# Attention over 4 images of 4096 positions: v's forms by halves of the channels, two products of the next step ahead of the second pair of banks, the projection one step behind

## The chip, the core and the metric

The kernel runs on one core of one Trainium2 chip. Its engines work side by side and wait for each other through semaphores: TensorE (PE) multiplies matrices, VectorE (DVE) and ScalarE (ACT) work on elements, GpSimd (POOL) and SyncE (SP) here mostly issue DMAs. TensorE writes its sums into eight PSUM banks; the other data lies in SBUF or, between stages, in DRAM. The metric is the device time of one execution in microseconds (us); three runs of the kernel before gave 2387.89, 2389.86 and 2392.86 us, median 2389.86.

## The reference

x is (4, 64, 64, 256), float32. Three projections give q and k with 128 channels and v with 256. Note that the results are only reshaped, not transposed, ahead of the attention, so a "channel" of the attention is a stretch of the flattened image.

```python
N = W * H                                   # 4096
q = jnp.einsum('bwhc,cd->bwhd', x, Wq) + bq # 128 channels
k = jnp.einsum('bwhc,cd->bwhd', x, Wk) + bk # 128 channels
v = jnp.einsum('bwhc,cd->bwhd', x, Wv) + bv # 256 channels
pq, pk, pv = (t.reshape(B, -1, N) for t in (q, k, v))
energy = jnp.einsum('bcn,bcm->bnm', pq, pk)
attention = jax.nn.softmax(energy, axis=-1)
out = jnp.einsum('bcm,bnm->bcn', pv, attention).reshape(B, W, H, C)
return gamma * out + x
```

## The kernel before

**Numbers in three forms.** Float32 data goes through TensorE as float32r. Each matrix is split into three forms, h (upper part), l (rest) and d (h scaled up a little, less the matrix). A product needs the d form's product, scaled by ScalarE, and on top the h and l forms' products. `split` (L153), `x_forms` (L212), `qk_forms` (L301) and `halves` (L389) make forms: ScalarE makes h, then VectorE d and l.

**Steps.** The attention of an image is cut into 8 groups (`NG`) of 512 columns n, and each group into 16 steps (`NU`) of two blocks of 128 rows m: 128 steps (`STEPS`) an image, 512 in all. The loop from L695 runs over these steps; n is the step, t its place in its group, b the image, and `late` says that the last image is reached (n >= 384). All instructions are put down by hand (the pools are under a manual schedule); each engine runs its own in that order. One iteration n issues, in this order:

- `cross(n + 2)` (L356): one matmul of the d forms for each of the two blocks (L362), scaled in its bank by ScalarE (L363). Two banks, tag "e", serve all steps.
- at t = 0, `upper(n + 1)`, ScalarE's h of the next step (L386), which the last step of a group leaves out; at t = 15, `sum_forms` (L455): ScalarE writes the h form zf of the group's sum (L460), VectorE its l form later (L462).
- ScalarE's part of a projection piece, `step(p, "act")`.
- `attend(n, 0)` (L422): six matmuls (L434). It multiplies v by the step's exps. j = 0 and 1 are the halves of the result's rows; each has a pair of PSUM banks, a (h and l forms) and b (d form), in which it adds up over the 16 steps of a group. So the first step of a group must find its four banks emptied.
- `energy(n + 2)` (L365): the h and l products on top of cross, four matmuls (L377), then ScalarE's exps (L380).
- `load_k(n + 5)` on POOL's queue and `store()` on SP's, which issues what is in the list `stores`.
- at t = 0 of images 0 to 2, `emptied(n - 1, 1)`: ScalarE copies the second pair of banks of the old group to SBUF (L448); at t = 15 `emptied(n, 0)` for the first pair. Otherwise `upper(n + 2)`.
- TensorE's part of the projection piece; at t = 0 `sums` of the old group (L472, two matmuls, and a copy by ScalarE, L473), and the generator `finish` (L475) is started, which each iteration takes one piece further: the sum to DRAM and back (SP, L480 and L482), its reciprocal at t = 3, back through DRAM, two operations of VectorE, at t = 8 a DMA on POOL's queue that adds x (L498), at t = 11 the store of the output on SP's queue (L502).
- `halves(n + 1)` on VectorE: the running sum (L397), l (L411) and d (L413); then VectorE's part of the projection piece.
- `attend(n, 1)`, six matmuls.
- at t = 6 a load of q, and at n = 115 to 130 of each image but the last a load of v of the next image into vall, which holds v for all 16 steps (`load_v`, L336), both on POOL's queue.

**Projection of the next image.** While an image is attended, the next one is projected in pieces (`step`, L563). 16 pieces r = 0 to 15 (`R`) serve one pair of blocks, 8 pairs an image; p counts the pieces, and r is p mod 16. r = 0: transposes; 1 to 4: forms of x; 5 and 6: products for q and k; 7 to 10: their forms; 9 to 12: products for v, first one half of its channels (eh = 0), then the other; 11 to 14: v's forms; 12 also loads the next x (SP). Each form is stored in DRAM by SP in the iteration after it is done: qk's after r = 8 and r = 10 (four DMAs of 192 KB each time), v's after r = 12 and r = 14 (two of 384 KB each time). At L714 p is n - 3 for n < 17, then two pieces an iteration for n = 17 to 23, then n + 4, so r = t + 4.

**Buffers that matter here.** The tag "pf" of the pool `work` has two buffers in turn: for the two forms of q and k, the two of v, and zf, five in each group. Whoever writes into such a buffer waits until the DMAs that store its old content are through. "o", the group's result before its store, has one buffer; "ld" (l and d) has two.

Of the kernel before, what the change touches and what calls it, by code (L numbers as in the profile page):

```python
# [9 lines left out]
F32 = mybir.dt.float32  # L10
F32R = mybir.dt.float32r
# [9 lines left out]
def kernel(  # L21
# [37 lines left out]
    B, W, H, C = x.shape  # L59
    P = 128  # L60
# [24 lines left out]
    NU = NM // 2  # L85
    STEPS = NG * NU
# [14 lines left out]
    with ExitStack() as fast:  # L101
# [4 lines left out]
        qkv = pool("qkv", 1)  # L106
        ppool = pool("ppool", 2)
        work = pool("work", 2)
        kpool = pool("kpool", 3)
        dram = pool("dram", 2, space=DRAM)  # L110
# [2 lines left out]
        ps_o = pool("ps_o", 1, space=PSUM)  # L113


        vall = qkv.tile([P, NU, 3, 2, C], F32R, tag="v", name="v")
        wf = qkv.tile([P, 2, 3, KC, C], F32R, tag="wf", name="wf")
        zd, rd = (dram.tile([B * NG, NB], F32, tag=n, name=n, bufs=1) for n in ("zd", "rd"))
        xs4 = work.tile([P, 4, 2, XB], F32, tag="o", name="xs", bufs=1)
# [25 lines left out]
        qd, kf, vf, units, loads, now = {}, {}, {}, {}, {}, {}  # L145
        active, stores = [], []
# [6 lines left out]
        def split(h, l, d, y):  # L153

            nc.scalar.activation(h, y, AF.Identity, scale=UPPER * E)  # L155
            yield
            for t, f in ((d, 1.0 / E + 1.0), (l, 1.0 / E)):
                nc.vector.scalar_tensor_tensor(t, h.bitcast(F32), -f, y, ALU.mult, ALU.add)  # L158
                yield
# [12 lines left out]
        def image(b):  # L172
            for g in range(NG):
                qd[b, g] = dram.tile([P, NJ, 3, P], F32, tag=f"qd{g}", name=f"qd_{b}_{g}")
            for t in range(NU):
                kf[b, t] = dram.tile([P, 2, 3, P], F32, tag=f"kf{t}", name=f"kf_{b}_{t}")
                vf[b, t] = dram.tile([P, 3, 2, C], F32, tag=f"vf{t}", name=f"vf_{b}_{t}")

        def bank(name, shape, b, ring):
            if b:  # L180
# [10 lines left out]
        def load_x(b, i):  # L191
            if b == B or i >= NI:
                return
            if b == 0:
                t = xs4[:, i % 4]
                if i:
                    nc.sync.dma_start(t, xv[b, i])
                loads["x", b, i] = t
                return
            pair = work.tile([P, 2, 2, XB], F32, tag="xd", name=f"x_{b}_{i}", bufs=1)  # L200
            for u in range(2):
                nc.sync.dma_start(pair[:, u], xv[b, i + u])
                loads["x", b, i + u] = pair[:, u]
# [115 lines left out]
        def v_forms(i):  # L319
            y = units.pop((1, 0, i))  # L320
            units.pop(("xf", 0, i))
            yield from split(vall[:, i, 0], vall[:, i, 1], vall[:, i, 2], y)

        def v_pair_forms(b, i, eh):
            y = units.pop(("v", b, i, eh))
            f = work.tile([P, 3, 2, C], F32R, tag="pf", name=f"vf{eh}_{b}_{i}")
            yield from split(f[:, 0], f[:, 1], f[:, 2], y)
            for u in range(2):
                stores.append((vf[b, i + u][:, :, eh, :], f[:, :, u, :]))

        def store():
            for to, f in stores:
# [3 lines left out]
        def load_v(b, t):  # L336
            nc.gpsimd.dma_start(vall[:, t], vf[b, t])
# [18 lines left out]
        def cross(n):  # L356

            if n >= B * STEPS:
                return
            for i in range(2):  # L360
                e = units["e", n, i] = ps_e.tile([P, NB], F32, tag="e", name=f"e_{n}_{i}")
                nc.tensor.matmul(e, *forms(n, i, 2), start=True, stop=False, skip_group_check=True)  # L362
                nc.scalar.mul(e, e, -REST)  # L363

        def energy(n):  # L365

            if n >= B * STEPS:
                return
            if n % NU:
                x = ppool.tile([P, 2, NB], F32, tag="x", name=f"x_{n}")  # L370
            else:
                x = ppool.tile([P, 2, NB], F32, tag="s", name=f"s_{n // NU}")
            units[n] = x
            for i in range(2):
                e = units.pop(("e", n, i))
                for f in range(2):
                    nc.tensor.matmul(  # L377
                        e, *forms(n, i, f), start=False, stop=(f == 1), skip_group_check=True
                    )
                nc.scalar.activation(x[:, i, :], e, AF.Exp, scale=(1.0 + E) ** 3 / E)  # L380

        def upper(n):
            if n >= B * STEPS:
                return
            h = ppool.tile([P, 2, NB], F32R, tag="h", name=f"h_{n}", bufs=3)
            nc.scalar.activation(h, units[n], AF.Identity, scale=UPPER)  # L386
            units[n] = units[n], h
# [34 lines left out]
        def attend(n, j, order=(0, 1, 2)):  # L422

            t = n % NU
            if t == 0:
                for i, c in enumerate("ab"):
                    pool, tag = ps_o, f"{c}{j}"
                    if j and n >= (B - 1) * STEPS and n // NU % 2 == 0:
                        pool, tag = now["banks"][i]
                    now[c, j] = pool.tile([P, NB], F32, tag=tag, name=f"{c}{j}_{n // NU}")  # L430
            for f in order:
                to = now["ab"[f == 2], j]
                for i in range(2):
                    nc.tensor.matmul(  # L434
                        to,
                        vall[:, t, f, i, j * P : (j + 1) * P],
                        units[n][f][:, i, :],
                        start=(t == 0 and i == 0 and f != 1),
                        stop=(t == NU - 1 and i == 1 and f != 0),
                        skip_group_check=True,  # L440
                    )
# [13 lines left out]
        def sum_forms(n):  # L455

            s = now["total"] = now["sum"]
            f = work.tile([P, 2, NB], F32R, tag="pf", name=f"zf_{n // NU}")
            h, l = now["z"] = f[:, 0, :], f[:, 1, :]
            nc.scalar.activation(h, s[:, 0, :], AF.Identity, scale=UPPER)  # L460
            yield
            nc.vector.tensor_tensor(l, s[:, 0, :], h.bitcast(F32), ALU.subtract)  # L462
            yield
# [231 lines left out]
        for n in range(B * STEPS):  # L695
            b, u = divmod(n, STEPS)
            g, t = divmod(u, NU)
            final = n == B * STEPS - 1
            if n == 0:
                image(1)  # L700
                load_x(1, 0)
            if u == STEPS - 5 and b + 2 < B:
                image(b + 2)
            if n == B * STEPS - 6:
                xr = ppool.tile([P, 2, NB], F32, tag="s", name="xr")
                nc.sync.dma_start(xr, xg[b, g])
            cross(n + LOOK)
            turn = t == NU - 1 and not final
            if t == 0 and n:
                upper(n + LOOK - 1)  # L710
            if turn:
                zf = sum_forms(n)
                next(zf)
            p = n - 3 if n < 17 else 2 * n - 20 if n < 24 else n + 4  # L714
            step(p, "act")
            if not final:
                attend(n, 0)
            energy(n + LOOK)
            load_k(n + LOOK + 3)
            store()  # L720
            late = n >= (B - 1) * STEPS
            if t == 0 and n:
                done = full
            if t == late and n > 1:
                emptied(n - 1 - late, 1, done)
            if turn:
                emptied(n, 0)
            else:
                upper(n + LOOK)
            step(p, "pe")  # L730
            if t == 2 * late and n > 2:
                sums(n - 1 - 2 * late)
                active.append(finish(n // NU - 1, now["o"], now["total"]))
            halves(n + 1)
            if turn:
                next(zf)
            step(p, "dve")
            if final:
                finish_last(n, xr)
                break  # L740
            attend(n, 1)
            full = now["a", 1], now["b", 1]
            if 17 <= n < 24:
                for engine in ("act", "pe", "dve"):
                    step(p + 1, engine)
            if t == 6 and n + NU < B * STEPS:
                load_q(*divmod(n // NU + 1, NG))
            if n >= STEPS - NU + 3 and (n - 3) // NU % NG == NG - 1 and (n - 3) // STEPS + 1 < B:
                load_v((n - 3) // STEPS + 1, (n - 3) % NU)
            proceed()  # L750
# [5 lines left out]
    with tc.If(nc.values_load(again[0:1, 0:1]) > 0), ExitStack() as general:  # L756
# [3 lines left out]
        xpool, xtpool, qkv = pool("gx", 2), pool("gxt", 2), pool("gqkv", 1)  # L760
        ppool, work = pool("gp", NP + 2), pool("gw", 1)
# [86 lines left out]
        for b in range(B):  # L848
# [16 lines left out]
            for g in range(NG):  # L865
                ps = []
                mx = work.tile([P, 2, NB], F32, tag="mx", name=f"gmx_{b}_{g}")
                for t in range(NP):
# [9 lines left out]
                    p = ppool.tile([P, 2, NB], F32, tag="p", name=f"gp_{b}_{g}_{t}")  # L878
# [54 lines left out]
                for s in range(2):  # L933
                    y = work.tile([P, NB], F32, tag="y", name=f"gy_{b}_{g}_{s}")
# [33 lines left out]
```

## Time and profile before

| | |
|---|---|
| median of 3 runs | 2389.86 us |
| the profiled execution's own time | 2388.01 us |
| its span | 2385.8 us |
| mean granted clock of TensorE | 0.997 |
| DVE busy | 2128.5 us (89%) |
| ACT busy | 1861.9 us (78%) |
| DMA queue q0 (POOL's issues) | 280.67 MB, 44.1% of the 16 engines' span |
| DMA queue q1 (SP's issues) | 130.77 MB, 16.1% |

How to read the profile's lines: a group of instructions is given by its line in the kernel, engine, operation and "output<-input", then shapes and count, busy us, mean ns of one, and the idle time of its engine just ahead of it with what ended it. In the rows in order of time the first two numbers are the start and the duration in us, and the bracket is idle time ahead. A row of the view by stretches has the stretch and its length, then the busy us of PE, PE's weight loads, DVE, ACT and POOL (with counts), TensorE's granted clock, the DMA engines' busy share and GB/s. A row of the chain of waits has start, duration and what the time went to. A matmul of 512 columns is listed with some 390 ns, but the next one starts 227 ns later, since they overlap.

### The profile page before, as it was taken

What the parts mean: (1) busy time and instruction counts of PE and PEld (TensorE: products, weight loads), DVE (VectorE), ACT (ScalarE), POOL (GpSimd) and SP (SyncE); (2) the same over time, 40 slices, a digit from 0 to 9 for tenths busy, and PEclk for the clock granted to TensorE, in tenths of its full rate; (3) what the DMA queues carried; (4) which work ended last, traced back from release to release, by engine and by line L of the source; (5) the groups of instructions that cost most, each with busy time, mean ns of one, the idle gap of its engine ahead of it and who ended that gap; (6) DMA issues with size and microseconds to landing.
All of it is one profiled execution on the core that took longest, in us unless ns stands there. A gap on an engine that the chain in (4) does not pass through costs nothing.

```text
span 2385.8 us, 31624 instructions
## 1 busy us (share of the span) xinstructions
PE 2341.1 (98%) x10844; PEld 1944.8 (82%) x10844; DVE 2128.5 (89%) x2114; ACT 1861.9 (78%) x3042; POOL 355.7 (15%) x642
## 2 busy tenths in 40 slices
PE   9999999999999999999999999999999999999998
PEld 9877888888878888888887888888888888888887
DVE  8988999889888899988988889999899888888888
ACT  7777878778777787877877778777787788887885
POOL 1101111111211111111121111111112111111110
PEclk9999999999999999999999999999999999999999
DMA  8456665556875666555688456665569644444453
GB/s 277 152 146 178 184 183 146 138 163 190 285 234 144 171 184 183 152 137 160 188 296 250 135 158 185 183 168 146 144 179 331 189 126 120 128 130 112 132 135 95
DMA packets 210382, 413.81 MB, mean 173 GB/s; under 512 B 26851, under 2 KB 114151, under 8 KB 210214
## 3 DMA queue, kind: packets, MB, share of 16 engines
q0 software_dynamic: 94272, 280.67, 44.1%
q1 hardware_dynamic: 115390, 130.77, 16.1%
q8 instruction: 89, 1.46, 0.3%
q14 instruction: 79, 0.65, 0.1%
q10 hardware_dynamic: 552, 0.26, 0.0%
HBM read 306.64 MB, written 104.98 MB: 173 GB/s over the span
## 4 chain that ended last, share of the span: by engine, by line
PE 86%; ACT 7%; DMA 4%; DVE 2%; issue 1%; SPq 0%; POOL 0%; ACTq 0%; DVEq 0%; POOLq 0%
PE a L434 35%; PE b L434 17%; PE e L377 17%; PE e L362 9%; PE qv L247 4%; PE v L264 2%; ACT x L380 2%; ACT o L448 2%; DMA out_dram<-o 2%; ACT e L363 1%; ACT h L386 1%; PE xt L210 1%; DMA qd<-f 1%; DMA o<-in_x_dram 0%; DVE ld L413 0%
## 5 line engine op out<-in xcount | busy, mean ns | idle before, releaser
L380 ACT ACTIVATE x<-e 128x512 f32<-128x512 f32 x960 | 522.2, 596 | 315.2 <-PE e L377 315.2
L411 DVE TENSOR_TENSOR ld<-x,h 128x1024 fp32r<-128x1024 f32 x480 | 585.4, 1220 | 109.8 <-ACT h L386 57.5
L397 DVE TENSOR_TENSOR s<-s,x 128x1024 f32<-128x1024 f32 x480 | 586.1, 1221 | 96.9 <-ACT x L380 93.9
L434 PE MATMUL a<-h,v 128*128 128x512 f32 x2048 | 637.1, 392 | 27.4 <-ACT o L448 27.4
L363 ACT ACTIVATE e<-e 128x512 f32<-128x512 f32 x1024 | 547.2, 573 | 132.5 <-PE e L362 132.1
L434 PE MATMUL b<-ld,v 128*128 128x512 f32 x2048 | 631.6, 390 | 0.2
L434 PE MATMUL a<-ld,v 128*128 128x512 f32 x2048 | 631.7, 390 | 0.0
L413 DVE SCALAR_TENSOR_TENSOR ld<-h,x 128x1024 fp32r<-128x1024 f32 x480 | 584.4, 1217 | 0.0
L349 POOL DMA_DIRECT2D k<-kf x512 | 272.6, 532 | 1969.0 <-PE e L377 1804.9
L377 PE MATMUL e<-q,k 128*128 128x512 f32 x2048 | 550.0, 390 | 2.4 <-ACT e L363 1.2
L386 ACT ACTIVATE h<-x 128x1024 fp32r<-128x1024 f32 x480 | 510.9, 1064 | 13.3
L434 PEld LDWEIGHTS a<-h,v 128*128 128x128 f32 x2048 | 377.9, 188 | 110.7 <-ACT o L448 38.2
L377 PEld LDWEIGHTS e<-q,k 128*128 128x128 f32 x2048 | 383.2, 188 | 86.6 <-ACT e L363 7.8
L434 PEld LDWEIGHTS b<-ld,v 128*128 128x128 f32 x2048 | 384.4, 188 | 82.2 <-DVE ld L413 1.1
L434 PEld LDWEIGHTS a<-ld,v 128*128 128x128 f32 x2048 | 384.7, 188 | 81.0
L362 PE MATMUL e<-q,k 128*128 128x512 f32 x1024 | 316.4, 390 | 0.9 <-ACT x L380 0.8
L362 PEld LDWEIGHTS e<-q,k 128*128 128x128 f32 x1024 | 191.9, 188 | 42.5 <-ACT x L380 2.3
L311 DVE SCALAR_TENSOR_TENSOR f<-f,qv 128x512 fp32r<-128x512 f32 x128 | 85.5, 678 | 1.2 <-ACT f L308 0.7
L247 PE MATMUL qv<-wf,xf 128*128 128x256 f32 x576 | 80.1, 287 | 2.5 <-DVE xf L229 2.3
L247 PEld LDWEIGHTS qv<-wf,xf 128*128 128x128 f32 x576 | 75.3, 193 | 5.8 <-DVE xf L229 2.5
L158 DVE SCALAR_TENSOR_TENSOR vf<-vf,v 128x512 fp32r<-128x512 f32 x96 | 65.2, 680 | 7.7 <-ACT vf L155 7.7
L411 DVE TENSOR_TENSOR ld<-s,h 128x1024 fp32r<-128x1024 f32 x32 | 39.2, 1226 | 20.1 <-ACT h L386 19.1
(91 smaller groups left out, 1125.2 us busy)
## 6 DMA issues: line engine op xcount, KB each, us to landing
k<-kf POOLq DMA_DIRECT2D x512, 384.0 KB, 3.5
vf<-vf SPq DMA_DIRECT2D x96, 384.0 KB
v<-vf POOLq DMA_DIRECT2D x48, 768.0 KB, 8.3
kf<-f SPq DMA_DIRECT2D x128, 192.0 KB
qd<-f SPq DMA_DIRECT2D x128, 192.0 KB
q<-qd POOLq DMA_DIRECT2D x31, 768.0 KB, 6.6
o<-in_x_dram POOLq DMA_DIRECT2D x31, 512.0 KB, 8.2
out_dram<-o SPq DMA_DIRECT2D x31, 512.0 KB
```

The costliest lines, as they stand in the source:

```text
L247: nc.tensor.matmul(to[:, s, :], left, right.rearrange("p s a -> p (s a)") if w else right, start=(f == 2 and s == k == 0), stop=(f == 1 an ...
L311: nc.vector.scalar_tensor_tensor(f[:, :, :, j, :], h.bitcast(F32), s, y, ALU.mult, op)
L349: nc.gpsimd.dma_start(t, kf[b, u % NU])
L362: nc.tensor.matmul(e, *forms(n, i, 2), start=True, stop=False, skip_group_check=True)
L363: nc.scalar.mul(e, e, -REST)
L377: nc.tensor.matmul(e, *forms(n, i, f), start=False, stop=(f == 1), skip_group_check=True)
L380: nc.scalar.activation(x[:, i, :], e, AF.Exp, scale=(1.0 + E) ** 3 / E)
L386: nc.scalar.activation(h, units[n], AF.Identity, scale=UPPER)
L397: nc.vector.tensor_tensor(s, s, x, ALU.add)
L411: nc.vector.tensor_tensor(l, x, h.bitcast(F32), ALU.subtract)
L413: nc.vector.scalar_tensor_tensor(d, h.bitcast(F32), 1.0 + E, x, ALU.mult, ALU.subtract)
L434: nc.tensor.matmul(to, vall[:, t, f, i, j * P : (j + 1) * P], units[n][f][:, i, :], start=(t == 0 and i == 0 and f != 1), stop=(t == NU - ...
```

## The change

It has three parts. First, v and its forms are laid out with the half of the channels ahead of the form, in vall, in the buffer in which the forms are made and in DRAM. Second, in the first step of a group (t = 0, images 0 to 2, not n = 0) the four matmuls of the h and l forms of step n + 1 into the first pair of banks are issued ahead of attend(n, 1); step n + 1 then issues only its d products there. Third, the piece p of the projection is n - 3 for n < 7, n - 2 for n = 7 to 17 and n - 1 from n = 18 on; only n = 6 and n = 17 run two pieces. From n = 18 on, r is t - 1 (15 at t = 0). Up to L715 the lines keep their numbers, so all that the profile names inside the helpers stay as they are.

```diff
-        vall = qkv.tile([P, NU, 3, 2, C], F32R, tag="v", name="v")
+        vall = qkv.tile([P, NU, 2, 3, C], F32R, tag="v", name="v")
...
-                vf[b, t] = dram.tile([P, 3, 2, C], F32, tag=f"vf{t}", name=f"vf_{b}_{t}")
+                vf[b, t] = dram.tile([P, 2, 3, C], F32, tag=f"vf{t}", name=f"vf_{b}_{t}")
...
         def v_forms(i):
             y = units.pop((1, 0, i))
             units.pop(("xf", 0, i))
-            yield from split(vall[:, i, 0], vall[:, i, 1], vall[:, i, 2], y)
+            yield from split(*(vall[:, i, :, f] for f in range(3)), y)

         def v_pair_forms(b, i, eh):
             y = units.pop(("v", b, i, eh))
-            f = work.tile([P, 3, 2, C], F32R, tag="pf", name=f"vf{eh}_{b}_{i}")
-            yield from split(f[:, 0], f[:, 1], f[:, 2], y)
+            f = work.tile([P, 2, 3, C], F32R, tag="pf", name=f"vf{eh}_{b}_{i}")
+            yield from split(*(f[:, :, j] for j in range(3)), y)
             for u in range(2):
-                stores.append((vf[b, i + u][:, :, eh, :], f[:, :, u, :]))
+                stores.append((vf[b, i + u][:, eh], f[:, u]))
...
                     nc.tensor.matmul(
                         to,
-                        vall[:, t, f, i, j * P : (j + 1) * P],
+                        vall[:, t, i, f, j * P : (j + 1) * P],
                         units[n][f][:, i, :],
...
-            p = n - 3 if n < 17 else 2 * n - 20 if n < 24 else n + 4
+            p = n - 3 + (n > 6) + (n > 17)
             step(p, "act")
-            if not final:
+            late = n >= (B - 1) * STEPS
+            if t == 1 and n > 1 and not late:
+                attend(n, 0, (2,))
+            elif not final:
                 attend(n, 0)
             energy(n + LOOK)
             load_k(n + LOOK + 3)
             store()
-            late = n >= (B - 1) * STEPS
...
+            if t == 0 and n and not late:
+                attend(n + 1, 0, (0, 1))
             attend(n, 1)
             full = now["a", 1], now["b", 1]
-            if 17 <= n < 24:
+            if n in (6, 17):
                 for engine in ("act", "pe", "dve"):
                     step(p + 1, engine)
```

## The prediction

> **What bounds the kernel now.** I read the page first, then the list of waits, then the rows in order of time around one start of a group, then the stretches that differ from it.
>
> ```profile
> PE 2341.1 (98%) x10844; PEld 1944.8 (82%) x10844; DVE 2128.5 (89%) x2114; ACT 1861.9 (78%) x3042; POOL 355.7 (15%) x642
> ...
> PE 86%; ACT 7%; DMA 4%; DVE 2%; issue 1%; SPq 0%; POOL 0%; ACTq 0%; DVEq 0%; POOLq 0%
> ...
> L434 PE MATMUL a<-h,v 128*128 128x512 f32 x2048 | 637.1, 392 | 27.4 <-ACT o L448 27.4
> ```
>
> TensorE is the bound: it is idle for 2385.8 − 2341.1 = 44.7 us. Of these 27.4 us stand ahead of one group, the h products of attend, and ScalarE's emptying of the banks (L448) ends them. No matmul is added or taken away, so only idle time and a lowered clock can be won.
>
> ```profile
> PE a L434 <- ACT o L448: 27.4, 25, 4.7
> ...
> ACT vf L155 <- DMA qd<-f: 7.8, 4, 2.8
> ...
> ACT o L448 <- DMA out_dram<-o: 7.1, 2, 5.1
> ```
>
> The columns are total, times and longest: 25 waits, one of 4.7 us. ScalarE itself waits twice for the store of the output (7.1 us). An ordinary start of a group, n = 176, in order of time:
>
> ```profile
> 886.96 0.62 PE L362 MATMUL e<-q,k 128*128 128x512 f32 x2
> ...
> 888.42 0.62 ACT L460 ACTIVATE zf<-s 128x512 fp32r<-128x512 f32 x1
> ...
> 889.43 1.09 ACT L380 ACTIVATE x<-e 128x512 f32<-128x512 f32 x2 [0.39 <-PE e L377]
> ...
> 891.04 0.62 PE L362 MATMUL e<-q,k 128*128 128x512 f32 x2
> ...
> 892.53 1.08 ACT L386 ACTIVATE h<-x 128x1024 fp32r<-128x1024 f32 x1
> ...
> 893.65 1.23 DVE L411 TENSOR_TENSOR ld<-x,h 128x1024 fp32r<-128x1024 f32 x1 [1.39 <-ACT h L386]
> 893.77 0.63 PE L472 MATMUL z<-zf,ones 128*128 128x512 f32 x2
> ...
> 894.48 0.69 ACT L448 ACTIVATE o<-a,gam 128x512 f32<-128x512 f32 x1
> ...
> 895.05 0.70 ACT L448 ACTIVATE o<-b,gam 128x512 f32<-128x512 f32 x1
> 895.23 0.73 PE L434 MATMUL a<-h,v 128*128 128x512 f32 x2 [0.82 <-ACT o L448]
> ...
> 896.57 0.56 ACT L473 COPY s<-z 1x512 f32<-1x512 f32 x1
> 896.72 0.61 PE L362 MATMUL e<-q,k 128*128 128x512 f32 x2
> 897.14 1.07 ACT L363 ACTIVATE e<-e 128x512 f32<-128x512 f32 x2
> ...
> 898.53 1.07 PE L377 MATMUL e<-q,k 128*128 128x512 f32 x4
> ```
>
> Each step begins with the two matmuls of L362. The last step of the old group lasts 891.04 − 886.96 = 4.08 us for 18 matmuls, 0.227 each. The first step of the new one lasts 896.72 − 891.04 = 5.68 us; it has two more matmuls (sums, L472), so 4.53 us of work and **1.15 us lost**. From 889.43 to 897.14 ScalarE has no idle time of its own: exps, two emptyings, two of L363, h, two exps, two emptyings. The second pair of banks is its last item.
>
> **The early product order.** attend(n+1, 0, (0,1)) puts four matmuls, 0.91 us, between the sums and attend(n, 1); step t = 1 then issues only the d pair there. It needs two things. h of n+1 ends at 892.53 + 1.08 = 893.6, in time. l of n+1 is the VectorE row at 893.65, which had waited 1.39 us for that h; it ends at 894.88. The sums end at 894.23 (893.77 plus two matmuls), the h pair at 894.68, so the l pair waits until about 894.93: 0.25 us. attend(n, 1) then begins at 895.38, after the a bank is free (895.17, and the row at 895.23 was its release) and its b matmuls come well after 895.75. So the old wait ends before it is reached. What is late next: cross(n+3) falls at 895.38 + 1.36 = 896.74, as before, but only the d pair (0.45 us) now stands between it and energy(n+3), where six matmuls stood. The first product ends 0.39 later plus hand-over, ScalarE is free at 897.14, its rescaling of the first bank takes half of 1.07 and ends at 897.75 to 897.8. energy could go at 896.74 + 0.45 + 0.45 = 897.65 and waits to about 897.8, with 0.05 more for the second bank. Lost after the change: 0.25 + 0.2 = 0.45 us; gained 1.15 − 0.45 = 0.70 per start. Bounds: 0 lost (all 1.15 won), or 0.85 lost if every hand-over on the way h, l, PE and PE, ScalarE, PE takes 0.1 more (0.3 won). I take 0.70, since each end is a row's end. The branch runs at n = 16 to 368, 23 starts; without n = 16, 128 and 256, which have troubles of their own, 20 × 0.70 = **14.0 us** (6 to 23).
>
> **The projection's new place, early steps.**
>
> ```profile
> 142.32 4.33 DMA vf<-vf
> ...
> 146.76 0.60 ACT vf L155
> ...
> 148.96 1.19 PE a L434 x4
> ...
> 181.22 6.63 DMA qd<-f
> ...
> 189.10 1.21 PE e L377 x4
> ```
>
> ```profile
> 120.00:180.00 60.00, 56.35 (x263) 46.43 (x261) 51.65 (x55) 45.62 (x76) 6.85 (x13) 1.00 0.50 145
> 180.00:240.00 60.00, 57.96 (x268) 47.43 (x268) 51.54 (x52) 45.23 (x75) 7.58 (x14) 1.00 0.62 178
> 780.00:840.00 60.00, 59.18 (x276) 49.22 (x275) 53.12 (x54) 47.40 (x79) 8.01 (x14) 1.00 0.56 157
> 660.00:720.00 60.00, 54.51 (x242) 44.75 (x241) 48.30 (x49) 42.36 (x70) 9.61 (x17) 0.94 0.75 224
> 1260.00:1320.00 60.00, 57.58 (x264) 47.81 (x265) 52.86 (x53) 45.92 (x75) 9.62 (x17) 1.00 0.80 236
> 1800.00:1860.00 60.00, 59.86 (x264) 49.12 (x263) 54.43 (x52) 48.48 (x80) 16.25 (x31) 1.00 1.07 370
> ```
>
> The chain shows that at 142 and 181 ScalarE's L155 waits for stores to leave the ring of two "pf" buffers. The second wait comes from the doubled steps 17 to 23, in which a buffer is asked for one step after its store. The new rule doubles only n = 6 (DVE pieces) and n = 17 (an empty piece and transposes), so that wait goes. The first stays: zf of n = 15 is still put in between the first two v forms, whose second is asked for at n = 15 instead of 16, and waits for a store of 4.33 us. Idle in the two stretches is 3.65 + 2.04 = 5.69 us (the second column is PE busy); 0.82 of it is the start at n = 32, counted above, and I leave 2 us for the first wait. **2.9 us** won (0 to 4.5).
>
> **The projection's new place, every group.** Piece r falls on t = r + 1 instead of r − 4, with all its DMAs. zf, which ScalarE writes at t = 15, now takes the buffer of the first v form, whose two stores SP issues after VectorE's piece at t = 13; before it had eight steps. That is the added wait, and ScalarE's exps, emptyings and the next rescalings are queued behind it.
>
> ```profile
> 881.35 0.68 DVE L229 SCALAR_TENSOR_TENSOR xd<-xf,xt 128x512 fp32r<-128x512 f32 x1
> ```
>
> This piece at t = 13 stands where the new one will; it ends at 882.0, two issues follow within 0.65 us, and zf goes at 888.42, with 0.39 us of idle behind it. The store has 888.8 − 882.65 = 6.2 us. The rows above give 4.33 us for such a store and 6.63 for one in a fuller queue. I take no wait; bounds 0 and 0.4 us × 23 = 9 us lost.
>
> **The layout.** vall and the forms exchange two axes: the store of a form's half has 128 runs of 3 KB, not 384 of 1 KB. The forms are written in two runs of 256 columns. L311 already writes in runs of 128:
>
> ```profile
> L311 DVE SCALAR_TENSOR_TENSOR f<-f,qv 128x512 fp32r<-128x512 f32 x128 | 85.5, 678 | 1.2 <-ACT f L308 0.7
> ...
> L158 DVE SCALAR_TENSOR_TENSOR vf<-vf,v 128x512 fp32r<-128x512 f32 x96 | 65.2, 680 | 7.7 <-ACT vf L155 7.7
> ```
>
> 678 against 680 ns: nothing. attend reads the same 128 columns.
>
> **The turns of image, n = 128, 256, 384.** Here 16 loads of v share the DMA engines with the stores.
>
> ```profile
> 643.93 24.08 DMA out_dram<-o
> ...
> 668.37 0.70 ACT o L448
> ```
>
> ```profile
> q0 software_dynamic: 1130, 4.64, 75.9%
> q1 hardware_dynamic: 1486, 1.63, 33.7%
> ```
>
> The second view is the queues' packets, MB and share from 644 to 660 us. Before, the output's store stood behind both v forms (1536 runs of 1 KB) on SP, took 24.08 us and stopped ScalarE until 668.37. The stretch from 660 lost 5.49 us idle and had the clock at 0.94, 0.06 × 60 = 3.6 us more: 9.1. The second turn lost 2.42, the third 0.14. After the change the output's store stands behind one q/k form (512 runs) and should be in time; but then the second q/k form, x and both v forms follow, and zf at n = 127 wants the first v form away within some 6 us. In q1's share, 1486 runs in 16 us or 93 a microsecond, the q/k form (512), x (512) and v form (256) are 1280 runs or 13.8 us from about 646, so 660 at best, 665 if larger runs take longer, against zf at 661. I put 5 us on the first turn, 4 on the second, and 1 on the third, which loads no x: 9.1 + 2.4 + 0.1 − 10 = **1.6 us** won (−14 to +10: all three as bad as the first was, or all as good as an ordinary start).
>
> The Trainium skill (DMA: Bandwidth & Descriptors, section Queues, rings and completion order) says that a DMA engine goes round its queues packet by packet, a packet being several descriptors. The near-equal counts of q0 and q1 agree; by it runs three times as long would carry three times the bytes a turn, which is rival B below.
>
> A stall here has a second price: the 0.94 above. The Trainium skill (TensorE: Matmul & The Clock Gate, section What's actually happening) says that about 3.4 us idle halves TensorE's clock; this trace's 4.7 us wait with its clock of 0.94 agrees, and by it a turn that still stalls that long keeps its 3.6 us.
>
> **Sum.** 14.0 + 2.9 + 1.6 = 18.5 us from the profiled execution's 2388.0 (span 2385.8): 2369.5. The median of the runs is 1.9 above that execution, so **2371 us**.
>
> **Rivals.**
> A, the sum above: 2371, alone 2361 to 2382. Chance 0.60.
> B, the turns clear as well, because the 3 KB stores leave in a third of the turns: 10 instead of 1.6, so 2363. For it: the packet counts. Against it: the DMA engines are already full there (75.9 + 33.7%), and the moved stores meet the end of the v loads. Chance 0.17.
> C, the change doesn't take the stall away: ScalarE's run from 889.43 to 897.14 remains, and the wait only moves to l and to energy. With 0.85 to 1.15 lost the starts give 0 to 6 us: 2379 to 2385. Chance 0.12.
> D, slower: zf waits at t = 15 of every group for the first v form's store. Each microsecond past the 6.2 above costs 23 us, and it decides from 18.5 / 23 = 0.8 us, a store of 7.0 us. At 8.2 us the time is 2371 + 46 = 2417. For it: 6.63 us in the early row; against it: the middle of a group has the DMA only half busy (0.56 in the row from 780). Chance 0.08. The other 0.03 is spread.
>
> This kernel's measurement can tell 0.2%, 4.8 us, from no change. A, B and half of C are faster: 0.83. The other half of C is the same, with a little of A and D: 0.09. D and the rest slower: 0.08. The range takes B in and the worse end of C: 2357 to 2386.
>
> **What would show it.** Right: the wait of L434 for L448 falls from 27.4 us to under 3; in its place small waits of L434 for L411 or L413 and of L377 for L363, 0.2 us each at 20 places; the busy PE in ordinary stretches rises from 59.18 to about 59.6; nothing at 181. Wrong: zf (L460) with idle time ended by the store of vf; a wait of L448 that stays; a lower clock in other stretches than now; stalls of k's loads behind the last loads of v.

## The result and the profile after

| | before | after |
|---|---|---|
| median of the runs | 2390.31 us (6 runs, 2387.76 to 2392.86) | 2381.43 us (6 runs, 2379.29 to 2382.37) |
| the profiled execution, its span | 2388.01, 2385.8 us | 2379.29, 2377.4 us |
| mean granted clock of TensorE | 0.997 | 0.996 |

The ratio is 0.9962, interval [0.9949, 0.9975]: 8.9 us faster, where some 19 us were forecast. The time lies inside the stated range of 2357 to 2386.

The page of the kernel after, busy time, the chain's shares, the queue of SP and the two groups of L434 on bank a:

```profile
PE 2353.2 (99%) x10844; PEld 1942.8 (82%) x10844; DVE 2134.5 (90%) x2114; ACT 1861.4 (78%) x3042; POOL 355.2 (15%) x642
...
q1 hardware_dynamic: 90814, 130.77, 15.7%
...
PE 88%; ACT 5%; DMA 3%; DVE 3%; issue 1%; SPq 0%; ACTq 0%; DVEq 0%
...
L434 PE MATMUL a<-ld,v 128*128 128x512 f32 x2048 | 634.7, 391 | 1.2 <-DVE ld L411 0.3
L434 PE MATMUL a<-h,v 128*128 128x512 f32 x2048 | 635.7, 392 | 0.1
```

The 27.4 us ahead of the h products are 0.1. TensorE is idle for 2377.4 − 2353.2 = 24.2 us, 20.5 less than before, yet the span is only 8.4 us shorter. The same 10844 matmuls are listed as 12.1 us busier. A matmul is listed with 390 ns though the next one can start after 227, so a wait of up to some 0.16 us between two of them shows no idle time at all, a longer one shows only its rest, and a lowered clock counts as busy too. Idle time alone does not tell the gain. The bytes of q1 are the same 130.77 MB. The list of waits of after (total, times, longest):

```profile
PEld e L377 <- ACT e L363: 19.9, 62, 0.6
...
ACT vf L155 <- DMA qd<-f: 12.4, 6, 3.3
...
PEld a L434 <- DVE ld L411: 10.5, 21, 0.7
ACT zf L460 <- DMA vf<-vf: 8.0, 3, 3.8
PE e L362 <- ACT x L380: 6.8, 4, 2.8
...
PEld a L434 <- ACT o L448: 1.8, 5, 0.4
```

The store of the output no longer stops ScalarE (it was 7.1 us), and the wait for L448 is nearly gone. New are the 21 waits for l, about one a start, the 62 for L363 (18 with 7.8 us before, so about two more a start), and three of zf for the store of a v form. A weight load's wait partly overlaps the matmul ahead, so these totals are not lost time.

An ordinary start, n = 176, after, in order of time:

```profile
880.21 0.62 PE L362 MATMUL e<-q,k 128*128 128x512 f32 x2
...
882.82 1.23 DVE L411 TENSOR_TENSOR ld<-x,h 128x1024 fp32r<-128x1024 f32 x1 [1.39 <-ACT h L386]
...
883.42 0.63 PE L434 MATMUL a<-h,v 128*128 128x512 f32 x2
...
884.10 0.73 PE L434 MATMUL a<-ld,v 128*128 128x512 f32 x2
...
884.67 0.63 PE L434 MATMUL a<-h,v 128*128 128x512 f32 x2
...
886.05 0.62 PE L362 MATMUL e<-q,k 128*128 128x512 f32 x2
...
886.48 1.07 ACT L363 ACTIVATE e<-e 128x512 f32<-128x512 f32 x2 [0.18 <-PE e L362]
886.51 0.61 PE L434 MATMUL b<-ld,v 128*128 128x512 f32 x2
887.11 1.23 PE L377 MATMUL e<-q,k 128*128 128x512 f32 x4
```

The early h pair starts at 883.42 and is issued by 883.87 (2 × 0.227 later). The l pair starts at 884.10, 0.23 late, when L411 is done (884.05). Its row shows no idle time ahead of it. It takes 884.67 − 884.10 = 0.57 to the next matmul, not 0.45: 0.12 more behind the wait. The d pair ends at 886.96, energy starts at 887.11, 0.15 late, and its four matmuls are listed with 1.23 us where an unbroken four has 1.08: the second bank was waited for too.

The two turns of image where it went wrong: ScalarE's rows of after, then rows of its chain of waits.

```profile
658.09 0.63 ACT L460 ACTIVATE zf<-s 128x512 fp32r<-128x512 f32 x1 [3.48 <-DMA vf<-vf]
...
1242.58 0.60 ACT L155 ACTIVATE vf<-v 128x512 fp32r<-128x512 f32 x1 [3.27 <-DMA qd<-f]
...
1250.02 0.63 ACT L460 ACTIVATE zf<-s 128x512 fp32r<-128x512 f32 x1 [3.80 <-DMA vf<-vf]
```

```profile
648.03 9.96 DMA vf<-vf
...
1237.24 12.67 DMA vf<-vf
```

The store of the first v form took 9.96 and 12.67 us, against a cover of some 6.2; zf at t = 15 waited 3.48 and 3.80 us for it, with the exps queued behind. TensorE's rows at the second turn:

```profile
1243.72 0.99 PE L362 MATMUL e<-q,k 128*128 128x512 f32 x2 [1.66 <-ACT s L380]
...
1251.19 1.28 PE L362 MATMUL e<-q,k 128*128 128x512 f32 x2 [2.78 <-ACT x L380]
```

TensorE stood idle there twice, each time for exps queued behind a wait of ScalarE: 1.66 us behind the wait of the second v form (L155) for q and k's stores, 2.78 us behind zf's. The view by stretches, after:

```profile
656.00:660.00 4.00, 1.64 (x6) 0.77 (x5) 1.29 (x4) 1.91 (x4) 0.89 (x2) 1.00 1.07 357
660.00:664.00 4.00, 4.00 (x11) 2.92 (x11) 2.35 (x4) 2.89 (x6) 0.00 (x0) 0.57 0.73 286
780.00:840.00 60.00, 59.95 (x271) 49.08 (x270) 54.64 (x55) 48.66 (x80) 7.40 (x14) 1.00 0.61 173
1248.00:1252.00 4.00, 1.22 (x4) 0.57 (x2) 1.32 (x3) 1.98 (x4) 0.38 (x1) 0.82 0.98 339
1252.00:1256.00 4.00, 4.00 (x10) 2.97 (x10) 2.35 (x3) 2.72 (x5) 0.00 (x0) 0.50 0.55 220
1256.00:1260.00 4.00, 4.00 (x16) 3.20 (x15) 2.34 (x2) 3.67 (x6) 1.06 (x2) 0.83 0.43 109
```

The turns show 2.4 and 2.8 us of idle TensorE (4.00 less the busy column), then a clock of 0.57, or of 0.82, 0.50 and 0.83: 4 × 0.43 = 1.7 us, and 4 × (0.18 + 0.50 + 0.17) = 3.4 us more. Some 0.3 of the 3.4 fell before TensorE went on at 1251.19 and cost nothing, which leaves 3.1. The two rows from 1252 have 10 and 16 matmuls, where 4 us at 0.227 each hold 17.6, and are 4.00 us busy all the same.

The next table cuts the executions at the same instructions: the distance between the starts of L362's first matmul of two steps, from the rows in order of time (us). A group is the mean of the ordinary groups of 16 steps in images 0 to 2; a turn is 32 steps around a change of image (112 to 143, 240 to 271, 368 to 399). One of the experiments below, zf_xf, stands beside them; the rest of the span differs by less than 1 us. Eight transposes (L210, 0.87 us where nothing interrupts them) that before has in steps 0 to 31 lie in the steps of turn 3 in the other two, since the projection runs later there.

| | steps 0 to 31 | group | turn 1 | turn 2 | turn 3 |
|---|---|---|---|---|---|
| before | 152.1 | 73.41 | 155.1 | 150.0 | 138.7 |
| after | 147.8 | 72.98 | 152.0 | 154.8 | 141.0 |
| after, zf in another buffer | 145.8 | 72.98 | 147.3 | 147.6 | 139.9 |

A group without any stall at its start would take 73.41 − 1.15 = 72.26 us.

### The profile page after: what moved, and what is told of

The parts are those of the page before. It is cut to its first block, busy times and chain, and to the rows that moved or that the text cites. A ratio compares the mean times of both kernels' runs of the same rounds, so it can differ in the third digit from the quotient of the medians.

```text
span 2377.4 us, 31567 instructions
## 1 busy us (share of the span) xinstructions
PE 2353.2 (99%) x10844; PEld 1942.8 (82%) x10844; DVE 2134.5 (90%) x2114; ACT 1861.4 (78%) x3042; POOL 355.2 (15%) x642
## 3 DMA queue, kind: packets, MB, share of 16 engines
q1 hardware_dynamic: 90814, 130.77, 15.7%
## 4 chain that ended last, share of the span: by engine, by line
PE 88%; ACT 5%; DMA 3%; DVE 3%; issue 1%; SPq 0%; ACTq 0%; DVEq 0%
PE a L434 35%; PE e L377 18%; PE b L434 18%; PE e L362 9%; PE qv L247 5%; PE v L264 2%; ACT x L380 2%; DMA vf<-vf 2%; DMA qd<-f 1%; ACT o L448 1%; DVE ld L411 1%; PE xt L210 1%; ACT e L363 1%; ACT h L386 1%; DVE ld L413 0%
## 5 line engine op out<-in xcount | busy, mean ns | idle before, releaser
L411 DVE TENSOR_TENSOR ld<-x,h 128x1024 fp32r<-128x1024 f32 x480 | 586.8, 1223 | 95.7 <-ACT h L386 49.5
L363 ACT ACTIVATE e<-e 128x512 f32<-128x512 f32 x1024 | 547.3, 573 | 137.1 <-PE e L362 136.9
L434 PE MATMUL a<-ld,v 128*128 128x512 f32 x2048 | 634.7, 391 | 1.2 <-DVE ld L411 0.3
L434 PE MATMUL a<-h,v 128*128 128x512 f32 x2048 | 635.7, 392 | 0.1
L434 PE MATMUL b<-ld,v 128*128 128x512 f32 x2048 | 632.2, 390 | 0.2
L377 PE MATMUL e<-q,k 128*128 128x512 f32 x2048 | 553.5, 392 | 1.1
L377 PEld LDWEIGHTS e<-q,k 128*128 128x128 f32 x2048 | 380.0, 188 | 95.6 <-ACT e L363 19.9
L434 PEld LDWEIGHTS a<-ld,v 128*128 128x128 f32 x2048 | 383.3, 188 | 89.9 <-DVE ld L411 10.5
L434 PEld LDWEIGHTS b<-ld,v 128*128 128x128 f32 x2048 | 384.7, 188 | 82.4 <-DVE ld L413 0.9
L434 PEld LDWEIGHTS a<-h,v 128*128 128x128 f32 x2048 | 379.8, 188 | 76.4 <-ACT o L448 1.8
L362 PE MATMUL e<-q,k 128*128 128x512 f32 x1024 | 318.8, 392 | 9.1 <-ACT x L380 6.8
L362 PEld LDWEIGHTS e<-q,k 128*128 128x128 f32 x1024 | 192.1, 188 | 54.1 <-ACT x L380 10.7
L411 DVE TENSOR_TENSOR ld<-s,h 128x1024 fp32r<-128x1024 f32 x32 | 39.2, 1226 | 30.0 <-ACT h L386 27.5
```

The costliest lines, as they stand in the source:

```text
L377: nc.tensor.matmul(e, *forms(n, i, f), start=False, stop=(f == 1), skip_group_check=True)
L411: nc.vector.tensor_tensor(l, x, h.bitcast(F32), ALU.subtract)
L434: nc.tensor.matmul(to, vall[:, t, i, f, j * P : (j + 1) * P], units[n][f][:, i, :], start=(t == 0 and i == 0 and f != 1), stop=(t == NU - ...
```

## The experiments

Every kernel here computes the whole function. The diffs are against the kernel after. Ratios are to the kernel before, run on the same chip (2389.4 us for the first four, 2387.6 for the next four, 2387.9 for the last two; 2390.3 beside after). So a difference in us between medians of different groups can be off by some 3 us; where it matters the profiled executions stand beside it.

**One part alone.** The early products, without the new place and the layout:

```diff
-            p = n - 3 + (n > 6) + (n > 17)
+            p = n - 3 if n < 17 else 2 * n - 20 if n < 24 else n + 4
...
-        vall = qkv.tile([P, NU, 2, 3, C], F32R, tag="v", name="v")
+        vall = qkv.tile([P, NU, 3, 2, C], F32R, tag="v", name="v")
```

> The kernel before with the early h and l products alone (old layout, old place of the projection). Theory: the early order is what shortens an ordinary start of a group; the pair of steps t = 0 and 1 goes from 5.67 + 5.06 us to about 10.3 us, a group from 73.41 to 72.98, as after the whole change; the first 32 steps stay near 152 us and the turns of image at n = 128 and 256 keep their waits for the output's store (24 and 21 us to land). 23 starts x 0.43: about 10 us faster, 2380. Rival: the ordinary gain comes from the projection's new place, and groups stay at 73.4 us, 2390.

Measured 2376.3 us, 0.9947 [0.9933, 0.9961], 13.0 us less than before and some 4 better than expected. Groups take 72.96, the same as in after, so the start does not care where the projection stands. The rest came at the first turn (155.1 to 151.2). In its waits

```profile
PE a L434 <- ACT o L448: 5.3, 3, 2.6
...
ACT o L448 <- DMA out_dram<-o: 5.0, 3, 3.0
```

the longest wait for the output's store is 3.0 us, not 5.1, and TensorE's 2.6, not 4.7.

The new place alone:

```diff
-            if t == 1 and n > 1 and not late:
-                attend(n, 0, (2,))
-            elif not final:
+            if not final:
...
-            if t == 0 and n and not late:
-                attend(n + 1, 0, (0, 1))
...
-        vall = qkv.tile([P, NU, 2, 3, C], F32R, tag="v", name="v")
+        vall = qkv.tile([P, NU, 3, 2, C], F32R, tag="v", name="v")
```

> The kernel before with the projection's new place alone. Theory: ordinary groups stay at 73.4 us (L434 still waits 0.82 us for L448), the first 32 steps go from 152.1 to about 148 us, and zf (L460) waits for the store of the first v form at the turns of image, longer than after the whole change (there 3.5, 3.8 and 0.7 us), since the store has 1 KB runs: 2390 to 2395. Rival: the waits of zf at the turns come from the early products or the layout, and without them the turns cost no more than before: 2386.

Measured 2394.4 us, 1.0025 [1.0012, 1.0038]: a loss of some 5 us. The first 32 steps are 4.0 us shorter (148.2), and the turns 9.4 longer together (155.3, 156.2, 141.7); 0.9 of either is the eight transposes. Its waits:

```profile
PE a L434 <- ACT o L448: 18.8, 23, 1.0
...
ACT zf L460 <- DMA vf<-vf: 12.2, 3, 5.6
PE e L362 <- ACT x L380: 10.8, 5, 4.6
```

Three waits of zf, one at each turn; the other 20 or so groups of images 0 to 2 show none, and the group's length is unchanged at 73.41. Nor does any row show L448 waiting for the output's store: the new place alone removes that stall. Rival D, a wait in every group, is ruled out.

The layout alone:

```diff
-            p = n - 3 + (n > 6) + (n > 17)
+            p = n - 3 if n < 17 else 2 * n - 20 if n < 24 else n + 4
...
-            if t == 0 and n and not late:
-                attend(n + 1, 0, (0, 1))
```

> The kernel before with the new layout of v's forms alone. Theory: nothing changes in ordinary groups (73.41 us), but at the turns of image the two v forms leave in 512 instead of 1536 runs, so that the output's store behind them lands sooner than 24 and 21 us and ScalarE's wait for it (7.1 us in all) goes: 5 to 10 us faster, 2381 to 2385. Rival: bytes and not runs decide, and nothing changes: 2390.

Measured 2380.8 us, 0.9968 [0.9957, 0.9979], 8.6 us less than before. Groups stay at 73.41. The turns are 8.1 us shorter, the first from 155.1 to 148.4, and the first 32 steps 1.6 longer in the profiled execution, whose clock was 0.66 from 148 to 153 us. Its waits have no row of L448 for the output's store any more: in the old place that store stood behind both v forms, and with 512 runs in place of 1536 ahead of it, it is away in time.

Early products and layout in the old place:

```diff
-            p = n - 3 + (n > 6) + (n > 17)
+            p = n - 3 if n < 17 else 2 * n - 20 if n < 24 else n + 4
...
-            if n in (6, 17):
+            if 17 <= n < 24:
```

> The change without the projection's new place: early products and new layout. Theory: the two gains add, groups of 72.98 us, no wait of zf for a v store, turns near an ordinary start, first 32 steps near 152 us: 2390 - 10 - 8 = 2372, better than the whole change (2381). Rival: the projection's new place is not what costs at the turns, and this is no better than 2381.

Measured 2371.8 us, 0.9933 [0.9912, 0.9953]: 9.6 us faster than all three parts together (7.5 between the profiled executions). So in this company the new place costs some 8 to 10 us. Between the two profiled executions the first 32 steps are 4.7 us longer here and the three turns 13.5 shorter (147.6, 147.3, 139.4).

Early products and new place, the old layout:

```diff
-        vall = qkv.tile([P, NU, 2, 3, C], F32R, tag="v", name="v")
+        vall = qkv.tile([P, NU, 3, 2, C], F32R, tag="v", name="v")
...
-            f = work.tile([P, 2, 3, C], F32R, tag="pf", name=f"vf{eh}_{b}_{i}")
+            f = work.tile([P, 3, 2, C], F32R, tag="pf", name=f"vf{eh}_{b}_{i}")
```

> The whole change without the new layout. Theory: in the new place the layout saves only part of zf's wait (12.2 us in all with 1 KB runs and without the early products, 8.0 us with both), so about 4 us slower than the whole change: 2385. Rival: the layout is worth in this place what it was in the old one, 8.6 us: 2390.

Measured 2383.9 us, 0.9987 [0.9973, 1.0001], with runs from 2378 to 2393. By the medians the layout is worth 2.4 us here, by the two ratios, each against the kernel before on its own chip, some 6: less than the 8.6 of the old place, where it saved the output's store, but by how much is not settled. In the profiled execution (2390.8 us) the waits show

```profile
ACT zf L460 <- DMA vf<-vf: 19.4, 3, 10.1
```

so without the longer runs the same store is later still, up to 10.1 us. Why it varies so much from run to run was not settled.

**Is it zf's buffer?** Two theories of the turns: zf waits for its ring, or the DMA engines are simply full and something else would be late in zf's place. zf gets a buffer that x's forms use, free since t = 13:

```diff
-            f = work.tile([P, 2, NB], F32R, tag="pf", name=f"zf_{n // NU}")
-            h, l = now["z"] = f[:, 0, :], f[:, 1, :]
+            f = work.tile([P, 2, KC, 2, 2, P], F32R, tag="xf", name=f"zf_{n // NU}", bufs=1)
+            f = f.rearrange("p f k u s a -> p f (k u s a)")
+            h, l = now["z"] = f[:, 0, :NB], f[:, 1, :NB]
```

> The whole change, but zf lies in the buffer of x's forms (tag xf), which is free from t = 13 to t = 2, and no longer in the ring of the v forms. Theory: the cost at the turns of image is zf's wait for the first v form's store; L460's wait (8.0 us) goes, the two groups around n = 128 and 256 fall from 152.0 and 154.8 to about 147.5 us each, around n = 384 from 141.0 to 139.5, ordinary groups stay at 72.98: about 13 us less than the whole change, 2368. Rival: the stores are late for everybody there, and the wait moves to the second v form (L155 waiting for q and k's stores, now 5.4 us at n = 256) or to the loads of k: 2376 or more.

Measured 2365.2 us, 0.9913 [0.9896, 0.9929], 16.2 us under after (14.9 between the profiled executions). ScalarE's rows at the second turn and one stretch of zf_xf (zf is written in line 461 there):

```profile
1234.27 0.60 ACT L155 ACTIVATE vf<-v 128x512 fp32r<-128x512 f32 x1 [0.76 <-DMA qd<-f]
...
1237.83 0.62 ACT L461 ACTIVATE zf<-s 128x512 fp32r<-128x512 f32 x1
```

```profile
1244.00:1248.00 4.00, 3.95 (x17) 2.88 (x17) 4.00 (x5) 3.50 (x7) 0.42 (x1) 1.00 1.02 371
```

zf has no wait, the clock stays at 1.00, and that with the DMA engines as full as before (1.02). The turns are 13.0 us shorter together, the first 32 steps 2.0. The theory of the ring holds. Full DMA engines alone cost little: L155 still waits for stores of q and k, 10.2 us in all, and TensorE stands idle behind that for 0.60 us at the first turn and 0.87 at the second. The edit also leaves the ring one use fewer in each group, which the run does not tell apart from zf's own wait; the shorter wait of L155 in the row above (0.76 against 3.27) is part of the gain.

**Is the rest of the start l's and energy's short cover?** cross(n + 3) goes between the early h and l pairs, which gives l 0.45 us and ScalarE's rescaling an earlier bank:

```diff
-            cross(n + LOOK)
+            if not (t == 1 and 1 < n < (B - 1) * STEPS):
+                cross(n + LOOK)
...
-                attend(n + 1, 0, (0, 1))
+                attend(n + 1, 0, (0,))
+                cross(n + 1 + LOOK)
+                attend(n + 1, 0, (1,))
```

> The whole change, with the two L362 matmuls of cross(n + 3) put between the early h pair and the early l pair instead of at the head of step t = 1. Theory: the 0.73 us that a start still loses are the wait for l, the short way from cross to energy, and TensorE's restart after each; with cross in between, l comes 0.45 us later and energy some 3 us after cross, so a group falls from 72.98 to about 72.4 us: 22 x 0.55, about 12 us less than the whole change, 2369. Rival: ScalarE's run of work decides, the wait moves to the emptied banks (L434 for L448) or to the banks of e (L362 for L380), and groups stay near 73 us.

Measured 2373.7 us, 0.9943 [0.9926, 0.9959], 7.7 under after (5.6 between the profiled executions). Groups fell to 72.68, not to 72.4. The same start in hoist:

```profile
885.03 1.07 PE L434 MATMUL b<-ld,v 128*128 128x512 f32 x4
885.03 0.56 ACT L473 COPY s<-z 1x512 f32<-1x512 f32 x1
885.50 1.04 ACT L363 ACTIVATE e<-e 128x512 f32<-128x512 f32 x2
...
886.12 1.20 PE L377 MATMUL e<-q,k 128*128 128x512 f32 x4
```

l is no longer waited for, but energy starts at 886.12, 0.18 behind the end of the b products (885.03 + 4 × 0.227 = 885.94). L363 begins only at 885.50, since the copy of the sums (L473) stands ahead of it on ScalarE.

Hoist with two more edits aims at both places at once: a projection four steps ahead of the group again (r = t + 4), reached by doubled steps that stand apart from the stores.

```diff
+        twice = (6, 17, 18, 19, 30, 31, 32)
...
-            p = n - 3 + (n > 6) + (n > 17)
+            p = n - 3 + sum(n > m for m in twice)
...
-            if n in (6, 17):
+            if n in twice:
```

> A version meant to beat both: early products, cross between them, the new layout, the projection in its old place (r = t + 4), reached by doubling at n = 6, 17, 18, 19, 30, 31, 32 only, where the pieces ask for no pf buffer. Theory: early products with the new layout gave 2371.8; cross in between saves 12, the smoother ramp 4: about 2356. Rival: the doubled pieces cost as much as before and cross in between saves nothing: 2372.

Measured 2360.4 us, 0.989 [0.9873, 0.9906], 4 us over what was expected. The turns are 146.8, 146.7 and 138.1; zf does not wait anywhere.

The other way to the same end, hoist with zf in the other buffer:

```diff
-            f = work.tile([P, 2, NB], F32R, tag="pf", name=f"zf_{n // NU}")
+            f = work.tile([P, 2, KC, 2, 2, P], F32R, tag="xf", name=f"zf_{n // NU}", bufs=1)
...
-                attend(n + 1, 0, (0, 1))
+                attend(n + 1, 0, (0,))
+                cross(n + 1 + LOOK)
+                attend(n + 1, 0, (1,))
```

> The whole change with both edits: zf in the buffer of x's forms, and cross(n + 3) between the early h and l pairs. Theory: the two costs are apart, at the turns and at the starts, so the gains add: 2365.2 less 20 x 0.30 us (a group went from 72.98 to 72.68 with cross moved) = 2359. Rival: with the turns cleared the loads and stores come closer together there and give some of it back: 2363 or more.

Measured 2358.1 us, 0.9879 [0.9863, 0.9896]: the two gains, 7.7 and 16.2, add up to 23.9, of which 23.3 came. (Between the profiled executions 5.6 and 14.9 would make 20.5, and 23.0 came.)

And on top of it the copy of the sums behind the two rescalings, here as a diff against hoist_zf_xf:

```diff
-            nc.scalar.copy(now["total"][0:1, 0, :], zp[0:1, :])
+            now["zp"] = zp
...
                 cross(n + 1 + LOOK)
+                summed_row()
                 attend(n + 1, 0, (1,))
```

> As the run beside it, and ScalarE's copy of the sum's row (L473) behind the two rescalings of cross(n + 3) instead of ahead of them. Theory: what a start still loses (72.68 - 72.26 = 0.42 us a group) is ScalarE's unbroken run, whose last items ahead of energy(n + 3) are that copy (0.56 us) and the rescalings; with the copy behind, energy waits about 0.3 us less: 72.4 us a group, some 6 us less than the run beside it, 2353. Rival: the 0.42 us are TensorE's restarts, which no order on ScalarE removes: no difference beyond 2 us.

Measured 2350.9 us (2349.9 to 2355.6), 0.9852 [0.9836, 0.9869]. This version beats both kernels, after by some 30 us. The same start in combo, where the copy is L479:

```profile
872.48 1.07 PE L434 MATMUL b<-ld,v 128*128 128x512 f32 x4
872.49 1.10 ACT L363 ACTIVATE e<-e 128x512 f32<-128x512 f32 x2
...
873.39 1.08 PE L377 MATMUL e<-q,k 128*128 128x512 f32 x4
873.47 0.57 ACT L479 COPY s<-z 1x512 f32<-1x512 f32 x1
```

L363 ends its first bank in time, energy starts at 872.48 + 0.91 = 873.39 without delay and runs through in 1.08. Groups take 72.38, 0.12 above the 72.26 of a start without a stall. ScalarE's L155 still waits 11.1 us in combo for stores of q and k, nearly as long as in after (12.4), and TensorE stands idle behind it for 0.75 us at the first turn and 0.82 at the second. So that wait is the smaller part of the price of the turns.

## Why the prediction was right or wrong

**The bound, the places and the sign: right.** TensorE's idle time ahead of L434 went, and the small waits of L434 for L411 and of L377 for L363 came at the places named. There is no wait for the ring at 181. Nothing waits in ordinary groups for zf's buffer, against rival D, and the output's store stops nobody. The busy time of an ordinary stretch rose past the 59.6 expected, to 59.95, because short waits are listed as busy. The time measured lies in the band of rival C, 2379 to 2385, by coincidence: C had a start losing 0.85 to 1.15 us, and it loses 0.72.

**The turns of image: wrong, and the step that failed.** "I put 5 us on the first turn, 4 on the second, and 1 on the third" was to give 1.6 us won. The three turns became 3.9 us longer. They hold three ordinary starts, each worth 0.43, and turn 3 the eight transposes, 0.9: the turns lost 3.9 + 1.3 − 0.9 = 4.3. Turn by turn the changes put were −4.1, +1.6 and +0.9 (5, 4, 1 less 9.1, 2.4, 0.1); measured, with the start's 0.43 and the transposes taken out, they were −2.7, +5.2 and +1.8. The mechanism was the one named: zf at t = 15, behind the store of the first v form, which was the prediction's own first sign of being wrong. What it cost was mis-sized. The three turns of after hold 3.2, 4.6 and 0.8 us of idle TensorE, 8.6 together, not far from the 5, 4 and 1 put; but the sum has no term for what the same part calls the second price. The clock took 1.7 and 3.1 us more, 4.8 together, and without these the turns would have won some 0.5, near the 1.6 put. Within that, the second turn was put below the first, although the same loads meet the same stores there: its store took 12.67 us, the longest, and the second v form's own wait, which the sum does not name, left TensorE idle for 1.66 us. zf_xf shows it from the other side: with zf's wait taken away, the clock's loss goes too. (The lower bound, three turns as bad as the first, is 11.6 − 27.3 = −15.7, not −14.)

**The start: the right mechanism, 8.6 us for 14.0.** Forecast 0.70 a start, measured 73.41 − 72.98 = 0.43, times 20. Still lost is 1.15 − 0.43 = 0.72, not 0.45: l's wait 0.23 (0.25 put), the l pair's restart 0.12 (none put), energy's first bank 0.15 and its second 0.15 (0.2 put for both), some 0.07 unaccounted. The lower bound had allowed 0.1 for every hand-over and held (0.3 won); the value taken let each wait end where the row of its releaser ends. Hoist and combo show it from the other side: l's cover brings 0.30, and the copy out of the way another 0.30.

**The early steps: 3.5 us for 2.9.** The first 32 steps are 4.4 us shorter, of which 0.9 are the eight transposes that went to turn 3, so 3.5 are won, inside the bounds of 0 to 4.5. What precedes them is 0.4 shorter, which is no gain of the change: step 0 begins anywhere from 68.5 to 71.5 us in the profiles of these kernels. The 2 us left for the first wait were right: zf_xf, which takes zf out of that ring, wins just 2.0 there.

**The layout: right in operations, and worth what its place makes of it.** VectorE's and TensorE's instructions are as long as before. The Trainium skill (DMA: Bandwidth & Descriptors, section Queues, rings and completion order) lets a DMA engine take turns between its queues packet by packet; by that rule longer runs carry more bytes a turn, as rival B had it. From 644 to 660 us the queues after are

```profile
q0 software_dynamic: 1084, 4.37, 75.5%
q1 hardware_dynamic: 1291, 1.93, 34.0%
```

so q1 moved 1.93 MB where it had moved 1.63, with 1291 runs for 1486. The trace agrees in direction, with 18% more and not three times as many. It is no clean test: much in q1 is no v form, and the two windows hold different stores. Nor are the counts that the prediction calls near-equal so near, 1130 and 1486. B as a whole fell, since the turns did not clear.

**Together.** 8.6 + 3.5 − 4.3 and the 0.4 ahead of step 0 make 8.2 us, against 2388.0 − 2379.3 = 8.7 between the profiled executions. Of what was missing from the 18.5 forecast, the turns account for 5.9 and the starts for 5.4. The parts alone, 13.0 and 8.6 won and 5.0 lost, would make 16.6: the layout won its 8.6 at the turns, with the stall of the output's store gone, and the new place removes that stall as well, so that gain is not there twice.

## What to carry to other kernels

Where a producer is moved, list who writes next into each of its buffers, and price the shortest distance from store to rewrite at the place where the DMA queues are fullest, with the clock's loss behind the stall in the sum. A stall taken from one place of a start is not won until the next hand-over is looked at: ask what stands on the other engine ahead of the instruction now waited for, and move the least urgent of it (here a copy of one row) behind. Parts that remove the same stall do not add up, so undo each part from the whole, and not only try each alone.

## What the runs showed of the hardware

**A short gap lowers the clock, sometimes.** Near the start at n = 16 early_layout has, in order of time and then by stretches,

```profile
149.73 0.73 PE L434 MATMUL a<-h,v 128*128 128x512 f32 x2 [1.76 <-ACT o L448]
```

```profile
150.00:152.00 2.00, 2.00 (x7) 1.55 (x7) 0.47 (x2) 1.63 (x3) 0.00 (x0) 0.69 0.00 0
152.00:154.00 2.00, 2.00 (x6) 1.59 (x5) 2.00 (x2) 1.07 (x2) 0.00 (x0) 0.50 0.03 2
```

and the kernel before has in the same two views

```profile
148.96 0.73 PE L434 MATMUL a<-h,v 128*128 128x512 f32 x2 [2.75 <-ACT o L448]
```

```profile
150.00:152.00 2.00, 2.00 (x10) 1.68 (x9) 1.27 (x2) 1.93 (x4) 0.00 (x0) 1.00 0.00 1
```

1.76 us of idle TensorE were followed by a clock of 0.69 and 0.50, while 2.75 us, before, left it at 1.00. In after the lowered clock was worth 1.7 us behind 2.36 us of idle time, and 3.4 behind 2.78. The Trainium skill (TensorE: Matmul & The Clock Gate, section What's actually happening) has a free-running window of about 3.4 us, and one idle window as what halves the clock. By that figure one and two windows at half speed cost an estimated 1.7 and 3.4 us, and the prices here agree; a free-running window also fits that the outcome varies. That it takes a whole idle window does not agree with drops behind 1.76 and 2.36 us.

**The same store can take two to three times as long at a turn.** In after the store of a v form took 4.64 us in the early steps (from 137.55), with the DMA engines busy to 0.66 from 136 to 144 us, and 9.96 and 12.67 us at the turns, with them busy to 1.09 and 1.07 from 648 to 658 and from 1237 to 1250. How much of it is the loads of v, and how much the stores of q and k still under way ahead of it in SP's queue, no run tells apart.
